# Attention's opening in a four-stage kernel: key ahead of query, adapter keys in four steps, later tiles' statistics after the first masks

## The chip, the cores and the metric

The program runs on one core of a Trainium2 chip. Its engines work side by side, each through its own queue in a fixed order: TensorE (PE in the profile, with its weight loads as PEld), VectorE (DVE), ScalarE (ACT), GpSimd (POOL) and SyncE (SP), whose queue here issues the DMA transfers. The metric is the device time of one execution in microseconds (us); a version is judged by the median of several executions.

## The reference

`x` is 4 x 256 rows of 512 floats. Four residual blocks follow each other: causal attention with an adapter, a clustered feed-forward block, a state-space block, and the feed-forward block again. The change is inside the first. Cut to that:

```python
qkv = einsum('btc,oc->bto', layernorm(x), w_attn)            # 32 heads of 16
q, k = rope(q), rope(k)
scores = q @ k.T / sqrt(16), causal;  y = softmax(scores) @ v
_, ak, av = adapter_wte (10 x 512) through the same weights   # 10 adapter rows
ascores = gating * softmax(q @ ak.T / sqrt(512))
x = x + (y + ascores @ av) @ w_proj.T
```

## The kernel before

The 1024 rows are eight tiles of 128 (`TT = 8`); a sample (`b`, four of them) is two tiles (`c` = 0 and 1). Every float32 product that has to be exact is three matmuls on rounded halves: `split` (L105-L108) makes a rounded copy on ScalarE and the remainder on another engine, and `mm3` (L110-L117) multiplies high by high, high by low and low by high. A projection of one tile is 12 matmuls of 512 columns.

**The opening.** SyncE loads tile 0 of `x`, a small constant, the four pieces of `wq`, tile 1, the attention constants `acon` (rotation tables, masks), then `wk`, `wv`, the other six tiles, the adapter rows `wte` and a few scalars. `prepared(0)` normalises tiles 0 and 1 (`normed`, L166 transposes), projects them (`projected`) and rotates the result (`rotated`: three VectorE products L323, L326, L327 and a GpSimd sum L329), in the order query 0, key 0, query 1, key 1, and then makes the two value projections (evicted into `av` at L431).

**Pieces.** `pieces(b, q, f)` takes eight heads of query (`f` = 0) or key (`f` = 1) of both tiles. GpSimd writes each as a rounded copy next to its remainder (`stacked`, a copy L342 and a subtraction L343, twice), TensorE transposes both (L444, tile `trp`), ScalarE evicts the transpose (L447, tile `pc`). For a key two DMAs then copy it with its rows swapped (`swapped`, L348). So a key is ready later than a query by that transfer. Pieces (0, 0) of query and key and the first half of the next query piece are made ahead of the loop.

**The loop.** One step `i` = 0 to 31 handles four heads (`u`) of a sample. TensorE's order is the program's order (`tc.manual_schedule`); the other engines' orders were put out by a scheduler that knows estimated times. In a step: 16 score matmuls (L492); VectorE masks them and takes the maxima (L500, eight instructions); ScalarE takes the exponentials (L508, eight); the projections that are due ("long"); the weighting of step `i - 2` (L533, L539); the transposes of step `i - 1`'s exponentials (L523, three groups, two evicted by ScalarE and one by VectorE, all at L524 into `eT`); the gathering of step `i - 3` (L553); then what is due as "turn", such as the transposes of a later sample's normalised tile (L166). The PSUM pool `ps` that all of these use has three buffers that go round, so that a transpose can have to wait for the eviction three tiles earlier.

**Work that is due.** A generator yields a stage and a step number; `step(stage, i)` resumes those whose number has come (`None` means the next step).

**The adapter.** `adapter_weights` (step 0, "long") projects the 10 adapter rows, stored as 80 columns, through `wk` (tile `pk`), and VectorE multiplies by a block pattern into `ak` (L364). `adapter_keys(ak)` (step 1, "turn") makes four groups: for each, GpSimd and VectorE write the copy and remainder of `ak` into the two stack buffers of the keys (L342, L343), TensorE transposes them (L376, four small transposes, tile `tra`), ScalarE evicts them into `akbd` (L380, two copies). `adapter_scores(b, q)` multiplies a query piece by group `q` (L457, four matmuls), evicted at L462 and turned back at L466 and L467. `adapter_values` projects the adapter rows through `wv` (tile `pv`).

**The output weights.** `wproj` comes in two DMAs of 512 KB (L297) into one buffer with the tag `ya`, which `wte_s` held before; each is split by two ScalarE copies and two GpSimd subtractions (tile `wp`).

**Statistics.** `norm.stats(t)` is two VectorE instructions (L138, L139) for a tile. Those of tiles 2 to 7 stand ahead of the loop, pinned in program order, and are followed by `norm.root(2, TT)`, one square root on ScalarE (L143, with a table load; the exponential needs another one) and a reciprocal (L144).

## Time and profile before

| what | value |
|---|---|
| runs | 1802.36, 1804.76, 1805.3 us; median 1804.76 us |
| the profiled execution | 1805.61 us; its span 1803.8 us |
| mean granted TensorE clock | 0.989 |
| busy share of the span | PE 97%, DVE 79%, ACT 70%, POOL 13% |

The span runs from the first to the last instruction; the profiled execution's own time lies 1.8 us above it. The first steps of the loop can be told apart by where the score matmuls (L492) start:

| stretch of the profiled execution | us | PE busy us | granted clock |
|---|---|---|---|
| start to the end of step 0's scores, 0 to 35.55 | 35.55 | 25.44 | 0.91 |
| value and adapter projections, 35.55 to 43.06 | 7.51 | 7.51 | 0.76 |
| step 1, 43.06 to 52.75 | 9.69 | 5.90 | 0.83 |
| step 2, 52.75 to 65.41 | 12.66 | 12.47 | 0.86 |
| step 3, 65.41 to 71.86 | 6.45 | 6.45 | 1.00 |

A "granted clock" of 0.5 means that TensorE ran at half speed for the whole of a stretch. From step 3 on a step takes some 6.5 to 7 us and PE is busy nearly all the time.

### The profile page before, as it was taken

How to read it: one execution, taken by the hardware profiler on the slowest of the kernel's cores; microseconds unless marked ns; L12 is line 12 of the kernel's file. 1: busy time of each engine (PE TensorE's matmuls, PEld its weight loads, DVE VectorE, ACT ScalarE, POOL GpSimd, SP SyncE). 2: the span in 40 equal slices, each digit the busy share in tenths (PEclk: the TensorE clock that was granted, in tenths of full speed). 3: DMA queues.
4: the chain of work that ended last, by engine and by line, in shares of the span. 5: the costliest groups of instructions: out<-in, count | busy, mean ns of one | idle time of the engine just before them, and what ended most of it. 6: DMA issues, size and time to landing. Idle time of an engine off the chain costs nothing.

```text
span 1803.8 us, 33220 instructions
## 1 busy us (share of the span) xinstructions
PE 1745.7 (97%) x12862; PEld 1417.8 (79%) x12862; DVE 1427.7 (79%) x2523; ACT 1268.7 (70%) x2293; POOL 240.9 (13%) x249
## 2 busy tenths in 40 slices
PE   7999988899999999999999999999999999999998
PEld 6777767778877888888888888888888888888877
DVE  5676676889998788787878797878788878887777
ACT  5676684578887668766866686668667867777754
POOL 5332320111110111011110101110111101101100
PEclk8999999999999999999999999999999999999999
DMA  4000100122344234423433252325333433343231
GB/s 157 19 19 19 47 26 26 43 71 99 109 127 137 80 106 154 120 85 99 153 100 100 88 162 90 109 81 176 103 94 112 135 106 94 115 138 115 85 97 56
DMA packets 136941, 173.71 MB, mean 96 GB/s; under 512 B 12752, under 2 KB 78032, under 8 KB 136784
## 3 DMA queue, kind: packets, MB, share of 16 engines
q1 hardware_dynamic: 127712, 138.57, 25.5%
q10 hardware_dynamic: 9072, 33.03, 4.8%
q8 instruction: 101, 1.65, 0.4%
q14 instruction: 56, 0.46, 0.1%
HBM read 131.71 MB, written 35.65 MB: 93 GB/s over the span
## 4 chain that ended last, share of the span: by engine, by line
PE 76%; DVE 11%; ACT 8%; issue 3%; DMA 1%; POOL 1%; SPq 0%; ACTq 0%; DVEq 0%; POOLq 0%
PE pp L115 13%; PE pp L117 12%; PE pp L116 12%; PE pyy L1252 7%; PE pog L115 6%; PE pog L117 6%; PE pog L116 6%; PE trx L1233 3%; DVE acc L980 2%; ACT e L508 1%; ACT em L1213 1%; DVE em L1226 1%; PE pq L115 1%; PE ptr L523 1%; PE pq L117 1%
## 5 line engine op out<-in xcount | busy, mean ns | idle before, releaser
L115 PE MATMUL pp<-mx,w 128*128 128x512 f32 x1144 | 459.3, 401 | 0.0
L117 PE MATMUL pp<-mx,w 128*128 128x512 f32 x1144 | 446.8, 391 | 0.0
L116 PE MATMUL pp<-mx,w 128*128 128x512 f32 x1144 | 446.1, 390 | 0.0
L1285 POOL TENSOR_TENSOR sq<-sq,x 128x1024 f32<-128x1024 f32 x54 | 132.1, 2446 | 1177.7 <-ACT x L1284 1177.7
L117 PEld LDWEIGHTS pp<-mx,w 128*128 128x128 f32 x1144 | 214.7, 188 | 46.2
L115 PEld LDWEIGHTS pp<-mx,w 128*128 128x128 f32 x1144 | 214.8, 188 | 44.7
L980 DVE SCALAR_TENSOR_TENSOR acc<-pp,cw_s,acc 128x1012 f32<-128x1012 f32 (+2 forms) x192 | 244.5, 1274 | 4.3
L116 PEld LDWEIGHTS pp<-mx,w 128*128 128x128 f32 x1144 | 215.1, 188 | 40.5
L1226 DVE TENSOR_TENSOR em<-em,gm 128x1280 f32<-128x1280 f32 x128 | 189.5, 1489 | 72.1 <-ACT em L1221 72.1
L115 PE MATMUL pog<-wo,gh 128*128 128x512 f32 x512 | 201.2, 393 | 2.0 <-DVE x L1381 2.0
L117 PE MATMUL pog<-wo,gh 128*128 128x512 f32 x512 | 200.2, 391 | 0.9 <-DVE gh L1364 0.9
L116 PE MATMUL pog<-wo,gh 128*128 128x512 f32 x512 | 199.8, 390 | 0.0
L1236 DVE TENSOR_TENSOR xd<-trx,dt_t 128x512 f32<-128x512 f32 x128 | 82.4, 685 | 141.5 <-PE trx L1233 141.5
L1152 ACT ACT_TABLE_LOAD x63 | 80.8, 1283 | 139.1 <-DVE acc L980 138.9
L1443 ACT ACTIVATE gt<-pp 128x1024 f32<-128x1024 f32 x64 | 65.6, 1025 | 145.0 <-PE pp L117 145.0
L1252 PEld LDWEIGHTS pyy<-em,xd 64*64 64x64 f32 x4096 | 130.2, 133 | 44.2 <-issue 17.6
L1213 ACT ACTIVATE em<-r,end_t 128x128 f32<-128x128 f32 x512 | 163.1, 389 | 0.8
L1252 PE MATMUL pyy<-em,xd 64*64 64x256 f32 (+3 forms) x4096 | 157.8, 300 | 3.1 <-DVE em L1226 3.0
L115 PEld LDWEIGHTS pog<-wo,gh 128*128 128x128 f32 x512 | 96.3, 188 | 24.8 <-issue 2.8
L508 ACT ACTIVATE e<-e,nmx 128x256 f32<-128x256 f32 (+1 forms) x256 | 97.2, 448 | 24.3 <-DVE nmx L500 24.2
L117 PEld LDWEIGHTS pog<-wo,gh 128*128 128x128 f32 x512 | 96.4, 188 | 22.3 <-DVE gh L1364 2.1
L116 PEld LDWEIGHTS pog<-wo,gh 128*128 128x128 f32 x512 | 96.4, 188 | 19.5
(324 smaller groups left out, 3094.5 us busy)
## 6 DMA issues: line engine op xcount, KB each, us to landing
wr<-in_win_dram SPq DMA_DIRECT2D x144, 256.0 KB, 2.7
r<-cumd SPq DMA_DIRECT2D x256, 128.0 KB, 2.9
spill<-gb ACTq DMA_DIRECT2D x63, 512.0 KB, 2.8
gr<-spill SPq DMA_DIRECT2D x120, 256.0 KB, 3.4
wor<-in_wout_dram SPq DMA_DIRECT2D x64, 256.0 KB, 4.4
pc<-pc SPq DMA_DIRECT2D x32, 128.0 KB, 2.0
out_dram<-x SPq DMA_DIRECT2D x7, 256.0 KB, 2.3
x<-in_x_dram SPq DMA_DIRECT2D x1, 1536.0 KB, 9.0
```

The costliest lines, as they stand in the source:

```text
L115: nc.tensor.matmul(o, lh, rh, start=(first and k == 0), stop=False)
L116: nc.tensor.matmul(o, lh, rl, start=False, stop=False)
L117: nc.tensor.matmul(o, ll, rh, start=False, stop=(last and k == n - 1))
L508: nc.scalar.activation(es_[c][:, r, :], es_[c][:, r, :], AF.Exp, scale=-1.0, bias=tops[c][:, r : r + 1],)
L980: nc.vector.scalar_tensor_tensor(av[:, :, d:], pv[:, :, : L - d], cw_s[:, ch, tap : tap + 1], av[:, :, d:], ALU.mult, ALU.add,)
L1152: nc.scalar.activation(pair(x2).rearrange("p k u i -> p u k i"), acc.rearrange("p (u k i) -> p u k i", u=2, i=Q), AF.Silu,)
L1213: nc.scalar.activation(piece(e, j, c, 2 - c, 2), rv[:, j, 2:, :], AF.Exp, bias=end_t[:, 2 * j + c, h : h + 1],)
L1226: nc.vector.tensor_tensor(e, e, gm, ALU.mult)
L1236: nc.vector.tensor_tensor(xd[:, hs, :].rearrange("p c (h d) -> p c h d", h=2), tr.rearrange("p c (h d) -> p c h d", h=2), dt_t[:, hs, 2 * ...
L1252: nc.tensor.matmul(py[d, u, j * L + c * Q : (j + 1) * L].rearrange("p (k i) -> p k i", i=Q), xd[us, 4 * j + c, d], piece(es2[hh], j, c)[us ...
L1285: (nc.gpsimd if n < NB - 2 else nc.vector).tensor_tensor(sqs[g], sqs[g], x2, ALU.add)
L1443: nc.scalar.activation(gts[i], pp, AF.Silu)
```

## The change

Three edits, all in attention:

1. For sample 0 alone the key goes first: `wk` is loaded and split ahead of `wq`, the projections run in the order key 0, query 0, key 1, query 1, and the key's first piece is made ahead of the query's.
2. The adapter keys' stacks get buffers of their own (`sk0`, `sk1`), two each, and the four groups are made in steps 1 (two of them), 2 and 3. Their stacks are written one or more steps earlier: groups 0 and 1 at the end of step 0, group 2 in step 1, group 3 in step 2. `ak` moves to the buffer with the tag `ya`, so that the `wproj` loads, which use the same buffer, come after the last use of `ak`.
3. The statistics of tiles 5, 6 and 7, and with them the square root for tiles 2 to 7, move from ahead of the loop to after step 0's masks.

```diff
-            def stacked(src, f, n=P, engine=nc.gpsimd, first=0):
-                st = stacks[f][turn_at[f] % NS]
-                turn_at[f] += 1
+            def stacked(src, f, st=None, engine=nc.gpsimd, first=0):
+                if st is None:
+                    st = stacks[f][turn_at[f] % NS]
+                    turn_at[f] += 1
+                n = st.shape[0]
...
-                ak = p2.tile([80, NH, HD], F32, name="ak", tag="t1")
+                ak = p1.tile([P, 2, C], F32, name="ak", tag="ya")[:40, 0, :].rearrange("p (h d) -> p h d", h=NH)
...
-            def adapter_keys(ak):
-                for q in range(4):
+            def adapter_stacks(ak, q):
+                return [
+                    stacked(
+                        ak[:, q * 8 : q * 8 + 8, :], 1, p2.tile([40, 8, HD, 2], F32R, name=f"sk{i}"), engine, i
+                    ).bitcast(F32)
+                    for i, engine in enumerate((nc.gpsimd, nc.vector))
+                ]
+
+            def adapter_keys(st, qs):
+                for q in qs:
                     tr = ps.tile([P, 2, 2, 4 * NA], F32, name="tra", tag="m")
-                    for i, engine in enumerate((nc.gpsimd, nc.vector)):
-                        s = stacked(ak[:40, q * 8 : q * 8 + 8, :], 1, 40, engine, i).bitcast(F32)
+                    for i, s in enumerate(st[q]):
...
+                order = (0, 1) if b else (1, 0)
...
-                made(0, 0)
+                made(0, order[0])
...
-                made(0, 1)
+                made(0, order[1])
                 yield "long", r + 3
-                made(1, 0)
+                made(1, order[0])
                 yield "long", r + 4
-                made(1, 1)
+                made(1, order[1])
...
-            weights(wq_s, wq, "pc0", nc.vector)
+            weights(wk_s, wk, "pc0", nc.vector)
...
-            weights(wk_s, wk, "pc1", nc.vector)
+            weights(wq_s, wq, "pc1", nc.vector)
...
                 ak = adapter_weights()
-                yield "turn", None
-                adapter_keys(ak)
+                yield "turn", 0
+                st = {q: adapter_stacks(ak, q) for q in (0, 1)}
+                yield "turn", 1
+                adapter_keys(st, (0, 1))
+                st[2] = adapter_stacks(ak, 2)
                 yield "long", 2
                 asides.append(adapter_scores(0, 0))
                 next(asides[-1])
                 adapter_values()
+                for q in (2, 3):
+                    yield "turn", q
+                    adapter_keys(st, (q,))
+                    if q == 2:
+                        st[3] = adapter_stacks(ak, 3)
...
-            for t in range(2, TT):
+            for t in range(2, 5):
                 norm.stats(t, tc.keep_in_program_order)
-            norm.root(2, TT)
             begin(0)
-            for f in range(2):
+            for f in (1, 0):
                 for _ in pieces(0, 0, f):
                     pass
...
                     next(scoring)
+                    if not i:
+                        for t in range(5, TT):
+                            norm.stats(t, tc.keep_in_program_order)
+                        norm.root(2, TT)
```

The pieces of a sample are kept by name (`turned_[b, q][f]`) instead of by the order of making. As built, the changed kernel has the same number of matmuls, masks, exponentials, copies and DMAs; the orders of the engines differ from those of before only in the opening and in steps 0 to 3, and SyncE's queue only in this: `wk` ahead of `wq`, and the swaps of the first two key pieces ahead of the two `wproj` loads, which before stood one ahead of each swap.

More of the change, by code (lines that the diff above doesn't have):

```diff
@@ L361, in adapter_weights @@
                     [[v[:, k, :] for v in wk_s] for k in range(KC)])
-                ak = p2.tile([80, NH, HD], F32, name="ak", tag="t1")
+                ak = p1.tile([P, 2, C], F32, name="ak", tag="ya")[:40, 0, :].rearrange("p (h d) -> p h d", h=NH)
                 bdk = col("bdk")[:40].unsqueeze(1).unsqueeze(3).to_broadcast([40, NH // 4, 4, HD])
                 nc.vector.tensor_tensor(
-                    ak[:40].rearrange("p (b e) d -> p b e d", e=4),
+                    ak.rearrange("p (b e) d -> p b e d", e=4),
                     pk[:40].rearrange("p (b e d) -> p b e d", e=4, d=HD), bdk, ALU.mult,
@@ L368, in adapter_weights @@
                 return ak
-            def adapter_keys(ak):
-                for q in range(4):
+            def adapter_stacks(ak, q):
[7 more added lines that the diff above has]
+                for q in qs:
                     tr = ps.tile([P, 2, 2, 4 * NA], F32, name="tra", tag="m")
-                    for i, engine in enumerate((nc.gpsimd, nc.vector)):
-                        s = stacked(ak[:40, q * 8 : q * 8 + 8, :], 1, 40, engine, i).bitcast(F32)
+                    for i, s in enumerate(st[q]):
                         for j in range(2):
-                            nc.tensor.transpose(tr[:, i, j, :], s[:40, j * P : (j + 1) * P], ident[:40, :40])
+                            nc.tensor.transpose(tr[:, i, j, :], s[:, j * P : (j + 1) * P], ident[:40, :40])
                     for i in range(2):
@@ L449, in pieces @@
                     swapped(o[:, 1], o[:, 0])
-                turned_.setdefault((b, q), []).append(o)
+                turned_.setdefault((b, q), {})[f] = o
                 yield
@@ L481, in scores @@
             def scores(b, u):
-                qT, kT = turned_[b, u // 2]
+                qT, kT = (turned_[b, u // 2][f] for f in range(2))
                 es_ = [p2.tile([P, 4, (c + 1) * P], F32, name=f"e{c}", tag=f"e{c}") for c in range(2)]
```

## The prediction

> **What bounds the kernel now.** I read the granted clock first (0.989, one core), then the page's busy shares (PE 97%), then the first 72 us, which is where the two kernels' engine orders differ; from step 4 on they are equal, so only the time at which step 4 starts can move. PE sets the end there, and what it waits for ahead is found in the chain of waits over 0 to 66 us (start, us, what):

> ```profile
> 29.83 0.26 POOL st L342
> 30.16 0.47 POOL st L343
> 30.67 0.38 PE trp L444 x2
> 31.07 0.59 ACT pc L447
> 31.68 0.55 SPq L348
> 32.28 2.03 DMA pc<-pc
> 34.44 0.91 PE sc L492 x10
> ...
> 48.80 0.30 POOL st L342
> 49.17 0.47 POOL st L343
> 49.68 0.45 PE tra L376 x2
> 50.25 0.31 POOL st L342
> ...
> 52.82 1.05 PE sc L492 x13
> ```

> Two holes are to be seen: the key's swap (31.68 to 34.44), and the adapter's four groups handing one buffer round between POOL and PE (47.04 to 51.78). Each costs twice, since the clock falls after a hole. Busy time by stretch (start:end, us, PE, PEld, DVE, ACT, POOL busy, then granted clock):

> ```profile
> 28.70:32.15 3.45, 0.86 (x7) 0.67 (x6) 3.35 (x9) 1.15 (x2) 3.37 (x10) 1.00 0.39 110
> 32.15:35.55 3.40, 1.37 (x17) 1.08 (x16) 1.59 (x5) 2.14 (x3) 2.55 (x6) 0.53 0.32 122
> 35.55:38.97 3.42, 3.42 (x12) 2.74 (x12) 2.76 (x17) 3.38 (x7) 2.64 (x5) 0.50 0.33 98
> 284.80:288.20 3.40, 1.80 (x24) 1.08 (x16) 3.18 (x21) 3.40 (x11) 0.36 (x1) 1.00 0.04 10
> 288.20:291.60 3.40, 2.73 (x12) 2.32 (x12) 3.24 (x9) 0.73 (x2) 0.93 (x1) 0.52 0.00 0
> ```

> In stretches of 3.4 us the clock is halved after one in which PE was busy for 0.86 of 3.45, 1.37 of 3.40 or 1.80 of 3.40 (53%), and whole again after a full one; 2.35 of 3.50 (67%, at 298.4) did not halve it. Lastly the rows of the output weights and of step 2's end:

> ```profile
> 33.39 1.14 ACT L107 CAST wp<-ar 128x512 fp32r<-128x512 f32 x2 [1.74 <-DMA ar<-in_wproj_dram]
> 34.09 2.53 POOL L108 TENSOR_TENSOR wp<-ar,wp 128x512 fp32r<-128x512 f32 x2 [0.85 <-ACT wp L107]
> 36.65 0.33 SPq L297 DMA_DIRECT2D ar<-in_wproj_dram  x1
> 63.31 0.59 ACT L524 COPY eT<-ptr 128x512 f32<-128x512 f32 x1 [4.77 <-PE ptr L523]
> 64.19 0.58 ACT L524 COPY eT<-ptr 128x512 f32<-128x512 f32 x1 [0.29 <-PE ptr L523]
> 65.41 0.69 PE L492 MATMUL sc<-pc,pc 32*128 32x256 f32 x16
> ```

> The loads' data are used at 33.39 and 42.07, long before step 2's copies: today they cost nothing.

> **The change, part by part.** The times are those of the profiled execution, carried forward along the changed kernel's engine orders; the sum stands against its 1805.61 us, 0.85 above the median of 1804.76.

> *Names exchanged, to 28.2 us.* `wk` takes the places of `wq` in SP's queue (4 DMAs), on ACT (0.62 each) and on DVE (0.69 each). Same sizes: 0.

> *Key first.* POOL finishes the third stack at 28.16 and the fourth at 30.62 whatever they are. The key is now the third: eviction 28.68 to 29.26 where it ended at 31.65. From that end to the scores' second half is 34.44 - 31.65 = 2.79 us, so they start at 32.05 instead of 34.44 (the query's own eviction, to 31.65, is just ahead). Nothing stands before the swap on SP, as the weight load now comes after it. Score matmuls to 32.9; the next query transpose needs POOL's eight operations of 30.56 to 33.24, so the value projection starts at 33.6 instead of 35.83.

> *Clock.* 32.15 to 35.55 still runs at half speed (the hole of 28.76 to 30.67 stays), but it is filled now, so 35.55 to 38.97 does not. A 512-column matmul takes 0.43 us then and 0.23 otherwise: 4.5 + 19.5 of the 24 value and adapter projections end so that step 1's scores start at 33.6 + 1.95 + 4.5 + 0.23 = 40.28 instead of 43.06: **-2.8**.

> *Statistics.* Three fewer ahead of step 0's masks (0.8 each) and no table loads there: masks at 33.0 instead of 36.86. Worth nothing by itself, since PE is in projections until 40.28; their cover is those 24 matmuls. In step 1 the same work is uncovered. DVE: `ak` 40.39 to 41.07, then three statistics (2.4) with two stack copies and a subtraction between (0.7): masks 1 start at 44.15, not 43.78, and end at 46.9. The rest of DVE's queue (eT copy, the normalised tile 2) waits behind. ACT: root after the last statistic, 44.2 to 44.5, table load 1.28, exponentials from 45.8 instead of 44.24: 4 x 0.43, two eT copies 1.0 (47.55 to 48.55), four short exponentials 1.2, four `akbd` copies 0.75 (to 50.5), `axs` 0.6.

> *Adapter groups.* Two of four leave step 1, and the ring between POOL and PE is gone: their stacks are ready at 42.7. But PE's transposes need the buffers of the eT copies: 47.5 (DVE), 48.05 and 48.55 (ACT). So a hole from 42.6 to 47.5 takes the ring's place; step 2's scores start at 49.65 (half clock, as before) instead of 52.75: **-3.1**. Then DVE's `axs` half at 51.1 to 51.8, masks 2 at 51.8 (54.13 before); the adapter values on PE need ACT's `sa`, behind two exponentials, and start at 53.5 (56.11 before): -2.6. 24 matmuls later the weighting starts at 59.2 (61.83), and step 2's exponentials end at 56.3 (58.54).

> *The output weights.* They have moved behind the last use of `ak` (POOL and DVE write group 3 by 49.5): first load lands at 49.55 + 3.6 (29.78 to 33.39) = 53.2, ACT splits it after step 2's exponentials, 56.3 to 57.45, POOL 56.95 to 59.5 (2.53), then SP issues the second: 59.5 + 3.6 = 63.1. ACT's queue has this load's split **between** step 2's two eT copies, so the second copy, with the adapter copies behind it, waits: 63.7 to 64.2. PE's transposes want that buffer, then that of the first `as` copy (0.3): 64.55, 0.6 more, step 3's scores at 65.15 instead of 65.41: **-0.3**. The cover that hid the loads is gone, and 2.3 us of the gain with it. Behind the loads on SP stands only the third key's swap, not needed before step 4's scores; behind the subtractions on POOL the next rotation's sum, whose inputs come at 60.4.

> *Groups 2 and 3.* One more split (0.57) and two copies (0.4) stand ahead of `axs` on ACT: masks 3 at 67.0 instead of 66.75. Group 3's transposes need step 3's eT copy on DVE (to 71.75) and take 0.3: step 4's scores at 72.1 instead of 71.86: **+0.24**.

> The bold numbers are the standing shift at their place, so the last one is the sum, and from there PE is busy with equal work in both: 1805.61 + 0.24 = 1805.85, or on the median **1805.0 us**.

> **Two costs the trace leaves open.** The landing: a 512 KB load took 3.6 us, the 256 KB `wk` loads 6.8 behind others; I take 3.6, since only this load is then in flight. Each us more is a us of PE; less than 1.3 us would unbind it. The clock of step 3: PE is busy some 2.2 of 3.4 us in 59.4 to 62.85 and 2.0 in the next stretch (59 to 65%), between the 53% that halved it and the 67% that did not: 0 or 12 matmuls x 0.2 plus small ones, about 1.6 us. I take 0 as the nearer, and keep 1.6.

> [...]

> **Rivals.**
> A, the second load is not last. Then step 3's scores keep the -2.6 or so: 1804.76 - 2.5 = 1802.3. For it: the queue orders only show who follows whom, and DMA time alone has no row at that place. Against: five rows in series, all measured.
> B, the same wait, longer, **slower**: the load lands after 6.8, PE waits 3.2 more, and its clock halves after: +0.2 + 3.2 + 0.8 to 1.6 = 1809 to 1809.8. It passes the mark of 3.6 from a landing of about 5.5 us. Against: the only row of this load.
> C, the hole of step 1 closes too, with exponentials soon after masks 1, and no half clock follows in step 2: another 1.5 to 2 on A: 1800.6. Against: the table load stands right there.
> D, the edit is undone by an order: the key's swap waits behind other DMAs. Then -2.8 falls away and all of step 1 shifts with it: 1805.0 + 2.8 = 1807.8. Against: SP's queue has nothing ahead of it.

> **How the numbers follow.** Forecast 0.55 (its own range 1802.6 to 1807.1: runs lie from 2.4 below the median to 0.5 above, and 1.6 of half clock may come on top), A 0.22, B 0.09, C 0.07, D 0.07. A measurement can tell some 0.2%, 3.6 us, so faster means under 1801.2 and slower above 1808.4. Faster: C, a third of A, a little of the forecast: 0.17. Slower: B and some of D and of half-clock stretches: 0.13. Same: 0.70. Range 1800.8 to 1808.2: it takes in A, D and most of C, and leaves B out with the ends of the others.

> **What would show it.** Right: key eviction ending near 29.3; step 1's scores near 40.3; exponentials 1 after a table load at 45 to 46; ACT idle before a `wp` copy between two eT copies, ended by the DMA, at 63; step 4's scores near 72. Wrong: no such idle time (A), or step 4 later than 74 (B).

## The result and the profile after

The changed kernel takes 1809.02 us (median of 19 runs, 1806.56 to 1811.89); the kernel before, run beside it, 1805.49 (19 runs, 1799.89 to 1809.93). The ratio is 1.0022, 95% interval 1.0013 to 1.0032. Over all executions of this study the means are 1809.3 (27 runs) and 1805.1 (152 runs), 4.2 +- 0.4 us apart (here and below +- is one standard error). Forecast were 1805.0 and "no change"; the time lies above the range.

The opening of the profiled execution went as it was worked out. The chain of waits of the changed kernel over 22 to 50 us (start, us, what):

```profile
30.65 0.59 ACT pc L458
31.29 1.23 PE sc L503 x16
...
40.06 0.68 DVE ak L366
...
43.80 0.30 ACT ars L143
44.12 1.28 ACT L519
45.41 1.70 ACT e L519 x4
47.12 0.95 ACT eT L535 x2
```

The key's swap is gone from the chain (before: a DMA of 2.03 us ahead of the scores), the scores run in one piece, and the adapter's keys (`ak`) are made from 40.06 instead of 43.17. The root and the reload of the exponential table now stand at 43.80 to 45.40, the exponentials come at 45.41, and the copies that PE waits for follow. PE's timeline shows the two waits that were expected (the number in brackets is PE's idle time ahead):

```profile
46.98 1.37 PE L385 MATMUL tra<-con,sk 40*128 40x40 f32 x8 [4.53 <-DVE eT L535]
63.24 0.41 PE L385 MATMUL tra<-con,sk 40*128 40x40 f32 x4 [1.92 <-ACT eT L535]
```

and ACT's timeline the cause of the second, the split of the output weights between two `eT` copies:

```profile
59.78 0.59 ACT L535 COPY eT<-ptr 128x512 f32<-128x512 f32 x1 [3.48 <-PE ptr L534]
61.99 0.62 ACT L107 CAST wp<-ar 128x512 fp32r<-128x512 f32 x1 [1.63 <-DMA ar<-in_wproj_dram]
62.52 0.58 ACT L535 COPY eT<-ptr 128x512 f32<-128x512 f32 x1
```

Starts of the score steps in the two profiled executions, in us, beside what was worked out (the changed kernel's first scores ran 0.42 us ahead in this execution, because its loads landed sooner: the first weights at 7.52 us, 7.82 before, and a load of `wv` at 14.17, 14.65 before):

| | before | worked out | after |
|---|---|---|---|
| step 1's scores | 43.06 | 40.28 | 39.95 |
| step 2's | 52.75 | 49.65 | 49.32 |
| step 3's | 65.41 | 65.15 | 64.17 |
| step 4's | 71.86 | 72.1 | 71.31 |
| step 31's | 280.55 | | 280.05 |
| state-space stage, first matmul | 345.46 | | 346.56 |
| span | 1803.8 | | 1805.1 |

From step 4 to step 31 both run alike, 0.5 us apart. The 1.6 us that the changed kernel then loses lie between 301 and 340 us, 1.3 of them from 336 to 339, in instructions that the change does not touch. Busy time by stretch (start:end, us, PE, PEld, DVE, ACT, POOL busy, granted clock, DMA share, GB/s), before:

```profile
332.73:336.14 3.41, 3.41 (x14) 2.98 (x15) 2.73 (x5) 1.92 (x5) 2.75 (x3) 0.50 0.15 15
336.14:339.55 3.41, 2.52 (x14) 1.69 (x13) 2.44 (x9) 0.17 (x1) 1.83 (x5) 1.00 0.73 222
```

and after:

```profile
332.36:335.77 3.41, 3.21 (x13) 2.78 (x14) 2.61 (x6) 2.17 (x6) 2.49 (x3) 0.50 0.10 7
335.77:339.18 3.41, 3.41 (x15) 3.26 (x14) 1.30 (x5) 0.00 (x0) 2.05 (x6) 0.50 0.75 219
```

In these two traces the clock stands at 1.0 or at 0.5 and changes only at instants that lie a multiple of 3.41 us apart, which are called its raster below: up to 340 us it falls at 11.88, 32.36, 49.43, 230.33, 288.36 and 332.73 us before, and at 11.50, 31.98, 45.64, 229.96, 287.98 and 332.36 after. From the last of these on it stood at half for one stretch before, for two after. So one pair of traces shows a loss at a place that has nothing to do with the change. The experiments ask whether that is chance, and where the mean of 4.2 us is made.

### The profile page after: what moved, and what is told of

Read it like the earlier page. It is cut to its first block, busy times and chain, and to the rows that moved or that the text cites. A ratio compares the mean times of both kernels' runs of the same rounds, so it can differ in the third digit from the quotient of the medians.

```text
span 1805.1 us, 33205 instructions
## 1 busy us (share of the span) xinstructions
PE 1743.6 (97%) x12862; PEld 1416.0 (78%) x12862; DVE 1427.3 (79%) x2523; ACT 1268.3 (70%) x2293; POOL 241.0 (13%) x249
## 4 chain that ended last, share of the span: by engine, by line
PE 71%; DVE 13%; ACT 9%; issue 3%; DMA 2%; POOL 1%; ACTq 0%; SPq 0%; DVEq 0%; POOLq 0%
PE pp L115 12%; PE pp L117 12%; PE pp L116 12%; PE pyy L1274 7%; PE pog L115 5%; PE pog L116 5%; PE pog L117 5%; PE trx L1255 3%; DVE acc L1002 2%; ACT e L519 2%; DVE em L1248 1%; ACT em L1235 1%; PE pg L1192 1%; PE pq L115 1%; ACT L1235 1%
## 5 line engine op out<-in xcount | busy, mean ns | idle before, releaser
L1248 DVE TENSOR_TENSOR em<-em,gm 128x1280 f32<-128x1280 f32 x128 | 189.5, 1489 | 72.1 <-ACT em L1243 72.1
L1274 PEld LDWEIGHTS pyy<-em,xd 64*64 64x64 f32 x4096 | 130.3, 133 | 44.2 <-issue 18.0
L116 PEld LDWEIGHTS pog<-wo,gh 128*128 128x128 f32 x512 | 96.2, 188 | 19.4
```

Of the source, the lines that this page charges most:

```text
L116: nc.tensor.matmul(o, lh, rl, start=False, stop=False)
L1248: nc.vector.tensor_tensor(e, e, gm, ALU.mult)
L1274: nc.tensor.matmul(py[d, u, j * L + c * Q : (j + 1) * L].rearrange("p (k i) -> p k i", i=Q), xd[us, 4 * j + c, d], piece(es2[hh], j, c)[us ...
```

## The experiments

Each single run lists its mean granted clock; for a clock that stands at 1.0 or at 0.5, as in the two traces above, 2 x (1 - clock) x span gives the time that PE spent at half clock. All ratios are to executions of the kernel before that ran beside the row's own.

| run | what it is | ratio (95%) | mean us | half clock, us |
|---|---|---|---|---|
| e1 | before, again | 1.0003 (0.9993 to 1.0013) | 1805.0 | 35 |
| e2 | after, again | 1.0030 (1.0019 to 1.0040) | 1809.2 | 41 |
| e3 | before + key first | 0.9993 (0.9983 to 1.0002) | 1803.6 | 32 |
| e4 | after, `ak` in `y` | 1.0022 (1.0012 to 1.0031) | 1808.0 | 38 |
| e5 | e4, loads behind the swap | 1.0001 (0.9992 to 1.0010) | 1805.7 | 36 |
| e6 | after, statistics ahead | 0.9996 (0.9987 to 1.0005) | 1804.7 | 31 |
| e7 | after, two waits filled | 0.9993 (0.9984 to 1.0001) | 1804.3 | 24 |
| e8 | e5 filled | 1.0007 (0.9996 to 1.0018) | 1805.6 | 28 |
| d3, d6, d9 | after, delayed at step 4 | 1.0020, 1.0018, 1.0023 | 1808.5, 1808.1, 1809.2 | 40, 35, 34 |
| e9 | e5 + e6 | 0.9994 (0.9983 to 1.0004) | 1803.9 | 31 |
| e10, e11 | e9, before, late waits filled | 1.0000, 1.0012 | 1806.1, 1809.2 | 32, 39 |

Standard errors of the means are 0.4 to 0.9 us. The kernel before itself had means of 1804.5 to 1806.3 us beside the different rows, so differences in us between rows that did not run side by side are somewhat less sure than the errors given with them.

**The same two kernels again.**

> The kernel before, once more. Every theory: ratio 1.000 within 0.1%, so that a difference of 0.2% can be told. The trace tells how far two executions of one program lie apart stage by stage. Theory P (the place of the 3.4 us clock stretches differs by execution, and the change's 1.3 us of the profiled pair are such a difference, at 336 us): starts of the score steps agree with the first trace within 0.6 us, but somewhere from 284 us on a half-clock stretch is there in one trace and not in the other, worth 1 to 2 us each. Theory O (the opening itself loses on average, by half-clock stretches behind its holes): one trace of this kernel looks like the other up to 72 us, and the end differs by under 0.6 us.

> The changed kernel, once more. Theory P: step 4's scores start within 0.6 us of the same step in the trace of before taken beside it, counted from the first score matmul of each kernel's own beginning as in the first pair (71.3 against 71.9), and the ratio is 1.000 to 1.001. Theory O: step 4's scores start 2 us or more later than in before's trace, and the ratio is again 1.002. Theory L (the stack tiles added shift every later address, and some instructions get slower by it): no jump anywhere, a lag that grows along the whole span; the first pair speaks against it, with a constant lag of -0.55 us from step 4 to 275 us and of +1.1 from 345 to 1230 us.

e1: 1.0003, no difference, and the traces of one program agree to 0.4 us at the scores of steps 1 to 4, then come apart by 1.9 us at step 31 and 2.5 at the state-space stage, and by 1.6 at the end. Theory P is right about executions, and yet e2's ratio is 1.0030: the loss is not chance. Its trace has what the first one lacked. The stretches around step 3 of the first execution:

```profile
59.29:62.70 3.41, 1.84 (x16) 1.48 (x14) 1.49 (x4) 1.29 (x3) 1.28 (x2) 1.00 0.47 154
62.70:66.12 3.42, 2.88 (x32) 2.48 (x33) 1.84 (x2) 2.15 (x7) 3.30 (x5) 1.00 0.01 2
```

and of e2:

```profile
59.40:62.81 3.41, 1.64 (x15) 1.28 (x13) 1.29 (x3) 1.44 (x3) 1.43 (x2) 1.00 0.43 149
62.81:66.23 3.42, 3.03 (x27) 2.53 (x28) 1.33 (x3) 1.99 (x7) 2.40 (x2) 0.50 0.01 2
66.23:69.64 3.41, 3.41 (x11) 2.73 (x11) 2.20 (x16) 2.99 (x9) 1.39 (x4) 0.50 0.10 38
```

The raster of 3.41 us lies 0.1 us later, PE was busy 1.64 instead of 1.84 us of the stretch (48 and 54%), and the clock fell for two stretches: step 4's scores start at 73.92 instead of 71.31. A window of 3.41 us laid over the first trace at full clock holds under 50% of PE time, between those two shares, if it starts between 59.4 and 61.5 us; if each place had an equal chance that would be 2.1 / 3.41 = 62% of the executions (an estimate). Six traces hold this opening up to step 3 unchanged, with the wait ahead of step 3's scores in each (after, e2 and, below, c2, d3, d6, d9): the clock fell behind it in two, e2 for two stretches and d3 for one. The two whole traces of before show no such window between 50 and 220 us.

**One part alone, and the loads.**

```diff
-ak = p1.tile([P, 2, C], ..., tag="ya")     # e4, e5: of the changed kernel
+ak = p1.tile([P, 2, C], ..., tag="y")
-load(r, src[:, k : k + 2, :])              # e5 only
+tc.keep_in_program_order(load(r, src[:, k : k + 2, :]))
-if i == 3:
-    weights(wp_s, wproj, "ya", nc.gpsimd, p1)
+weights(wp_s, wproj, "ya", nc.gpsimd, p1)  # behind pieces(0, 0, f)
```

> Before, with the key ahead of the query for the first sample and nothing else. By the prediction's own steps: step 1's scores 2.8 us earlier than before (near 40.2), the ring of the adapter groups unchanged behind it, so step 2's scores near 50, weights' loads early as before, so step 3's and 4's scores keep 2 to 2.8 us: ratio 0.9985. Rival: the step behind swallows it (masks 1 or the adapter values end last), step 4's scores within 0.7 us of before's, ratio 1.000.

> The changed kernel, but the adapter keys stand in the buffer of y instead of that of ya, so the output weights' loads no longer wait for them. By the prediction's chain: step 2's scores as in the changed kernel (49.3), step 3's scores about 2 us earlier than there (near 62), step 4's near 69.3, ratio 0.9985 to 0.999 on before. Rival: the output weights' subtractions, on POOL again ahead of the adapter stacks, delay the transposes of the adapter groups by up to 5 us, and step 2's scores come at 52 or later: ratio 1.000 or above.

> The changed kernel with the adapter keys in y's buffer (as in e4) and the first load of the output weights queued on SP directly behind the first key's swap, so that neither delays the other. Theory W (the loss is the wait for the second load at step 3, and in e3 and e4 the load ahead of the swap): step 1's scores 40.0 to 40.6, step 2's 49.3 to 49.9, step 3's near 62.3, step 4's near 69.3, ratio 0.998 to 0.999. Theory H (the loss is the hole of step 1 itself, 4.5 us of idle PE behind statistics, root and table load, and the half clock behind it): the hole is there again from 42.4 to 47, mean half-clock time over the runs stays near 38 to 41 us where before has 35, ratio 1.001 or above as in e4.

e3 missed: step 1's scores come at 42.31, 0.75 earlier than before with all of the opening 0.74 ahead, so nothing is gained there. The chain of e3:

```profile
28.98 0.33 SPq L297
29.40 0.55 SPq L348
30.00 3.52 DMA pc<-pc
33.65 0.91 PE sc L494 x11
```

With the output weights' loads where they were, the first (L297, 512 KB) is issued 0.4 us ahead of the key's swap, and the swap takes 3.52 us instead of 2.03. e4 shows the same, 3.80, and gains nothing on the changed kernel that can be told (1.0022). So the change's moving of those loads behind `ak` is what lets "key first" work, and it is also what stalls step 3. e5 has both: swap off the path (step 1's scores at 39.87, clock back at 35.4), no wait at step 3 (63.28 with step 2's at 49.97, 13.3 us where the changed kernel has 14.9), step 4's at 70.33. It is 3.6 +- 0.7 us faster than the changed kernel in the mean, though its ratio of 1.0001 is not the 0.998 to 0.999 that theory W expected, and its trace has step 4 only 1.0 us earlier than the changed kernel's. So theory W holds for the wait, but the wait itself does not account for the 3.6; e5 does not beat before, and the hole of step 1 is still there.

**The statistics back ahead, and the waits filled.**

```diff
-for t in range(2, 5):                      # e6
+for t in range(2, TT):
     norm.stats(t, tc.keep_in_program_order)
+norm.root(2, TT)
...
+if i == 1:                                 # e7, e8, behind the turning
+    warmed(ps_y.tile([P, L], F32, name="idle", tag="py"), [ones] * 14)
...
+if i == 2:                                 # ahead of the adapter keys
+    warmed(ps_s.tile([P, 3, P], F32, name="idle", tag="sc")[:, 0], [ones] * 6)
```

> The changed kernel with the statistics of the later tiles and their root ahead of the first masks again, as before. Theory H: ACT's table load and DVE's three statistics leave step 1, so the copies that PE waits for come 2 us or more earlier and the hole of step 1 shrinks from 4.5 to under 3 us; step 2's scores near 47.5, and although the wait for the output weights stays, the ratio falls by 0.1% or more against the changed kernel, to 1.001 or 1.002. Theory W: the time is set by the second load, whose issue goes by the last read of the adapter keys, so step 3's scores move by under 1 us and the ratio stays at 1.002 to 1.003.

> The changed kernel with 14 small matmuls of ones ahead of PE's wait in step 1 and 6 ahead of its wait at the end of step 2, into banks that are free there; nobody reads them. Their only use is to keep PE busy. Theory C (what the change loses is half-clock stretches behind its two holes, at step 1 in every execution, at step 3 in those whose 3.4 us raster falls so): no half-clock stretch between 42 and 72 us in the trace, mean half-clock time over the runs 6 to 10 us less (near 32 to 35), ratio 1.000 or below. If the waits themselves are the loss and not the clock, the stretches vanish and the ratio stays at 1.002 to 1.003.

> e5 with the matmuls of ones of e7. Theories W and C together: step 4's scores near 67.5, no half-clock stretch between 42 and 72 us, ratio 0.997 to 0.998, and faster than e5 and e7. If e5 has shown that the wait for the output weights is worth nothing, as e7.

e6 went the way of theory H, and further than the 1.001 or 1.002 that it gave: the whole loss is gone (4.6 +- 0.5 us against the changed kernel) although the wait for the output weights is still there (1.88 us of PE, 1.92 in the changed kernel). ACT's timeline of e6 has no root and no table load in step 1:

```profile
42.92 0.91 ACT L519 ACTIVATE e<-e,nmx 128x256 f32<-128x256 f32 x2 [3.31 <-DVE nmx L511]
43.73 0.56 ACT L458 CAST pc<-trp 128x512 fp32r<-128x512 f32 x1
44.20 0.91 ACT L519 ACTIVATE e<-e,nmx 128x256 f32<-128x256 f32 x2
45.01 1.05 ACT L535 COPY eT<-ptr 128x512 f32<-128x512 f32 x2
```

The copies start at 45.01 instead of 47.02, PE's hole of 4.53 us becomes two of 1.81 and 0.71, and step 2's scores start at 47.11 instead of 49.32. So the third edit, which the prediction did not price by itself, costs the opening 2.2 us in these two traces.

e7 gave the largest gain, 5.0 +- 0.5 us against the changed kernel, and 17 us less half clock. But not where it was expected: its trace has half clock from 49.3 to 56.1 all the same, and its step 4 starts at 72.31, 1.0 later than the changed kernel's; the gain shows later, between step 31 and the state-space stage (63.3 us, 66.5 in the changed kernel). e8 was a miss: 1.0007, no faster than e5 or e7, with half clock from 51.1 to 57.9 in its trace. Filling the waits did not keep the clock up in these two traces.

**The opening by itself.** Four kernels were cut off behind step 7. What is left runs in the order of the whole kernels; PE and GpSimd have all their instructions, VectorE and ScalarE lack a few whose results only the later part uses (a normalisation near 65 us, and some of the adapter's from 93 us on). The kernels before and after lack the same ones.

```diff
+if i == 7:
+    break
...
+e = all_es[7][1].rearrange("p r i -> p (r i)").rearrange("p (t c) -> p t c", c=C)
+for t in range(0, TT, 2):
+    load(ov[:, t : t + 2, :], e)
```

> The kernel before, cut off behind step 7's weighting and transposes: sample 0's remaining attention, the other samples, the feed-forward and the state-space stage are left out, and step 7's exponentials are written to the output. Engine orders up to there are those of the whole kernel. Its time is the opening's own, with some 10 us of output behind it: about 110 to 125 us. It is the base for the other three; the ratio to the whole kernel says nothing.

> The changed kernel, cut in the same way. Theory O (all of the loss is made in the opening): median 4 us above c1. Theory S (the opening loses only where step 3 falls to half clock, in a part of the executions, and what is left of the 4 us comes from where the raster stands at the later holes): mean 1 to 1.7 us above c1, the single times in two groups some 2.6 us apart. The worked sum of the prediction: 0.2 above c1.

> e7 (the changed kernel with matmuls of ones ahead of the two waits), cut in the same way. e7's whole time lies 5.2 us under the changed kernel's. Theory O: c3 lies 5 us under c2. Theory S: 1 to 2 us under c2, since only step 3's half clock is taken away, and the rest of e7's gain is made later.

> e6 (the changed kernel with the statistics ahead again), cut in the same way. Theory O: 4.6 us under c2, as the whole kernels lie. Theory S: by the traces step 4's scores are 2 us earlier (69.3 against 71.3), and step 3 may fall to half clock here as well: 2 us under c2, and 0.5 to 1.5 under c1.

| | mean us, all executions | half clock, us | whole kernel, mean us | half clock, whole less cut |
|---|---|---|---|---|
| c1, before | 107.0 +- 0.8 (6) | 19.3 | 1805.0 | 15.8 |
| c2, after | 109.1 +- 0.7 (6) | 21.6 | 1809.3 | 19.6 |
| c3, e7 | 107.4 +- 0.6 (6) | 14.2 | 1804.3 | 10.1 |
| c4, e6 | 106.0 +- 0.1 (4) | 19.4 | 1804.7 | 11.7 |

The changed opening is 2.1 +- 1.0 us longer than before's, half of the 4.2 +- 0.4; the two shortest executions of each lie 2.5 us apart. That is two standard errors, so the opening's share is known only roughly. With the statistics ahead again (c4) the opening is 3.1 +- 0.7 us shorter than c2's, which is most of the 4.6 that e6 gained. Single times of c2 spread from 106.5 to 111.1 without two clear groups, so that part of theory S was not seen. Against the changed kernel, e7's opening is 1.7 +- 0.9 us shorter and the whole 5.0 +- 0.5: behind step 7, where the two run the same instructions in the same order, 3.4 +- 1.1 us are won. The last column shows the same in the clock: what follows is the same in all four, and it spends 10 to 20 us at half clock, by the opening that it follows.

**A pure delay.**

```diff
+if i == 4:
+    warmed(ps_s.tile([P, 3, P], F32, name="idle", tag="sc")[:, 0], [ones] * 6)
     scoring = scores(b, u)
```

> The changed kernel with 3 matmuls of ones (0.22 us each at full clock) on PE ahead of step 4's scores, 0.66 us in all; nobody reads them. Raster at any place with equal chance: mean span 0.7 us above the changed kernel's 1807.5, so 1808.2. Raster bound to the program's start: another mean by 1 us or more; by the traces, in which the time from step 4's scores to the state-space stage is 275.2 us where an edge lies 1.6 us behind those scores and 273.3 where it lies 1.0 behind, about 1806.5.

> The same with 6 (1.3 us). Equal chance: 1808.8. Bound: unlike 1808.8 by 1 us or more, in either direction, and not in line with d3 and d9.

> The same with 9 (2.0 us). Equal chance: 1809.5. Bound: unlike 1809.5 by 1 us or more.

The mean spans are 1806.7, 1806.3 and 1807.4 us where equal chance gives 1808.2, 1808.8 and 1809.5. Work that nobody needs, 1.3 us of it, made the kernel 1.3 +- 0.6 us faster: 2.6 +- 0.6 less than its own cost (d9: 2.1 +- 0.6, d3: 1.5 +- 0.7). The delay itself does arrive: in d6's trace step 4's scores start 8.68 us after step 3's, 7.14 in the changed kernel, and the time from there to step 16 is the same (92.9 and 92.8 us). A later wait that takes up part of the delay could explain a cost of nothing, as d3 and d9 have within their errors, but not a gain, and d6's gain is two standard errors. That what becomes of the delay is decided by where the next holes meet the raster is the reading that fits; the traces do not show it by themselves.

**Both repairs together, and the late holes.**

> The changed kernel with the later tiles' statistics and root ahead of the first masks again (as e6), the adapter keys in y's buffer, and the output weights' loads directly behind the first swap (as e5). By the chain: step 2's scores near 47.5 as in e6, no wait for the output weights, so step 3's near 60 and step 4's near 66.5, 5 us under the changed kernel's 71.3: ratio 0.9975 to 0.9985 against before. If the loads' place costs nothing once the hole of step 1 is short, as e6: 0.9996.

> e9 with matmuls of ones ahead of three late waits of PE: 8 at step 23, 6 in the turning of step 31, and 3 and 2 instead of one each ahead of the state-space stage's first and third transposes; nobody reads them. Theory R (half-clock stretches at the late holes, which fall by raster, give back what the opening gains): no half-clock stretch between 200 and 345 us, mean half-clock time over the runs under 20 us (e9: 30.6), mean span 4 to 5 us under that of e11, ratio 0.995 to 0.997. Rival: the late stretches have nothing to do with it (the opening is not that much shorter in most executions); e10 lies 1 us or less under e11.

> The kernel before with the same matmuls at the same three late places. By the traces, its stretches there are 13.7 to 17 us at half clock, worth 3 to 5 us: mean half-clock time near 20 (before: 35), ratio 0.998. If filling does not keep the clock, 1.000 or above.

e9 joins the edits of e5 and e6. Its trace does what its text says: step 2's scores at 45.57, step 4's at 66.33, 5.5 us ahead of before, and a time of 1797.54. But 2.3 of the 5.5 are there at the first scores (29.45, before 31.71): in this execution the clock did not fall near 12 us, as it did in before's (at 11.88). e10's trace, with the same opening, has step 4 at 68.16. And 1797.54 was e9's fastest execution; the others reach 1806.51, and the ratio is 0.9994 where 0.9975 to 0.9985 was expected, not told apart from 1. e5's and e6's gains do not add up: each alone wins back about the whole loss. e10 and e11 missed their first aim: the matmuls of ones at step 23 kept the clock there and lost it a little later. e9 around its late hole:

```profile
221.30:224.70 3.40, 0.73 (x5) 0.50 (x6) 2.07 (x5) 3.40 (x10) 1.11 (x1) 1.00 0.20 77
224.70:228.10 3.40, 3.40 (x30) 2.70 (x34) 2.31 (x14) 3.34 (x5) 3.37 (x5) 0.51 0.01 2
```

and e10, whose times are some 2 us later:

```profile
223.70:227.10 3.40, 2.96 (x30) 2.60 (x34) 1.76 (x6) 3.38 (x9) 1.64 (x2) 1.00 0.19 74
227.10:230.50 3.40, 2.73 (x44) 1.98 (x40) 2.01 (x9) 3.05 (x4) 3.40 (x5) 1.00 0.00 0
230.50:233.90 3.40, 1.72 (x12) 1.26 (x12) 2.83 (x16) 3.40 (x10) 0.51 (x2) 1.00 0.00 0
233.90:237.30 3.40, 3.16 (x26) 2.54 (x27) 0.28 (x2) 2.00 (x6) 0.00 (x0) 0.50 0.00 0
237.30:240.70 3.40, 3.40 (x19) 3.40 (x19) 2.13 (x16) 2.75 (x7) 1.40 (x4) 0.50 0.13 46
```

In e9 the hole halves the clock for one stretch in which ACT is busy throughout, so the slow PE delays little. In e10 PE keeps its speed, runs ahead of ACT (3.40 of 3.40 busy) and DVE, waits for them at 230.5 to 233.9, and is then slow for three stretches in which it has the most to do; from step 16 to step 31 e10 takes 120.7 us, e9 116.1. This is no chance of one pair: e11, with the same matmuls at step 23, takes 122.1, and the fourteen whole traces without them take 115.9 to 117.6. Up to 1.8 us of it may be the matmuls of ones themselves (8 x 0.22, an estimate; PE spent 1.95 us on those at step 23 in e10's trace). Between themselves e10 and e11 still answer: with the same late edits the short opening is worth 3.2 +- 0.9 us, where the traces' openings differ by 4.2 and e9 and before without late edits by 1.3 +- 0.9. No version here is faster than before with an interval below 1.

## Why the prediction was wrong

The schedule of the opening was worked out to within 1 us for the profiled execution; what failed are two steps about the clock behind it, a term taken as 0 and the statement that nothing changes from step 4 on.

*Names exchanged, key first, clock of step 1.* Right: scores 0 in one run, step 1's at 39.95 (worked out 40.28), one half-clock stretch instead of two. e3 adds what the prediction only noted in passing: the step needs the loads out of the swap's way. Rival D is what becomes of "key first" alone.

*Statistics.* The times were right (exponentials 1 worked out at 45.8, measured 45.41), the pricing was not. They entered the sum only as part of the hole that "takes the ring's place", with -3.1 for both together. By the prediction's own rows they put 2.4 us of VectorE work and 1.6 us of root and table load ahead of step 1's exponentials; e6 measured 2.2 us at step 2's scores, and c4 against c2 3.1 +- 0.7 for the opening. The table load itself cost what the sum gave it, 1.28 us (the last section has the rows).

*Adapter groups.* Right as a whole: hole from 42.45 to 46.98 (42.6 to 47.5), step 2's scores at 49.32 (49.65).

*The output weights.* Right: ACT idle before a `wp` copy between two `eT` copies, ended by the DMA, and step 3's scores at 64.17. PE's wait is 1.92 us, not 2.9, as the second load's data were there at 61.99 and not at 63.1. Rival A falls. Rival B has the measured time (1809 to 1809.8) but not its cause: it wanted a landing of 6.8 us, and the two loads took 3.5 and 3.8. That its number is met is luck, but for its last term, a half clock behind the wait.

*The clock of step 3.* **Here the prediction failed.** The prediction had PE busy 2.2 of 3.4 us and 2.0 in the next stretch (59 to 65%), took no half clock "as the nearer" and kept 1.6 us. PE was busy 1.84 and 1.64 us in the two executions, 54 and 48%: one raster, that of before's trace, was laid over the new schedule, and the whole came out some 0.9 us earlier against it, so that most of PE's wait fell into one stretch. Nor was the share a safe mark: in the changed kernel's first trace the clock fell after a stretch of 61% (2.08 us of 3.42, from 328.94) and held after one of 52% (1.78 of 3.41, from 342.60). In e2 it fell behind a single wait of 1.97 us. In the first execution the clock held all the same, so the 0 was right there; in e2 it fell and cost 2.6 us, not 1.6, since it stayed down for two stretches. The cut kernels put the whole opening at +2.1 +- 1.0 where the sum had +0.24. Two falls in six traces are worth under 1 us in the mean (an estimate: 2 / 6 of at most 2.6), so the step-3 clock alone need not be all of that, and what the rest is stays open.

*"From there PE is busy with equal work in both."* This second step failed too. The work is equal, the time is not: the shift at step 4 is not the shift at the end, and the likely reason is that it moves the holes at 227, 285 and 330 us against the clock's raster. That the time is not equal is plain in the traces: from step 4's scores to the state-space stage two executions of before take 273.6 and 276.3 us, the first two of the changed kernel 275.3 and 274.4, and over the fourteen whole traces without late matmuls of ones it is 270.5 to 276.3. e7 against the changed kernel (3.4 +- 1.1 us behind step 7) and d6 (2.6 +- 0.6) show it in means. Cut and whole kernels leave 2.0 +- 1.1 us of the loss to this step; that the raster accounts for just this remainder is argued, not shown.

*How much is the clock at all.* The changed kernel spends 41.3 us at half clock in the mean, before 35.3. A 512-column matmul takes 0.43 us at half clock and 0.23 at full clock (those at 34.44 and 35.87 in the changed kernel's trace), so the work of 6 us at half clock would take some 3 us at full clock, and slow matmuls account for some 3 us of the 4.2 at most (an estimate); the last 1 us or so is waiting, and the runs do not show where.

The range leaned on three runs of before, 2.9 us apart; 152 runs lie 10 us apart, and in e1 a run's time goes with its half-clock time (0.45 us for each us, correlation 0.9; in the changed kernel's 19 runs 0.33 and 0.7).

## What to carry to other kernels

Price each part of a change against the stage that it lands in, by itself: an edit that frees one place and fills another can spoil the whole, even where the sum of all parts looks like nothing; here taking one edit back (e6) won the whole loss back. Where the clock falls after a badly filled stretch, count PE's busy share for windows at every offset over the new schedule, not only along one execution's raster; here a new place, 54% full in one execution and 48% in another, was paid for in two of six traces. And when the effect sought is a few us of 1800, judge by the mean of many runs and their clocks: one trace can show the fastest execution of a kernel that is no faster.
